# A four-layer graph network on one core: the order of work from a table, layer 1's transposes moved off TensorE

## The chip, the cores and the metric

The kernel runs on one core of a Trainium2 chip. The metric is the device time of one execution in microseconds (us). Engines are named as the profile names them: PE is TensorE (PEld its weight loads), DVE is VectorE, ACT is ScalarE, POOL is GpSimd, and SP is SyncE, which here issues every DMA.

## The reference

64 independent graphs, each with 256 nodes of 256 features (`x`) and a dense 256 x 256 weighted adjacency (`adj`), all fp32, go through four layers. Each layer is followed by x = layernorm(x + layer(x, adj)).

```python
# layer 0, 4 heads of 64
X, q, k = heads(lrelu(x @ W_lin + b_lin)), heads(lrelu(x @ W_q)), heads(lrelu(x @ W_k))
adj_h = adj * sigmoid(q @ k.T / 8);  dis = rsqrt(adj_h.sum(-1))
y = layernorm(concat(dis[:, None] * adj_h * dis[None, :] @ X)) * ln_g + ln_b
# layer 1, 8 heads of 32
attn = softmax(where(adj > 0, q @ k.T / sqrt(32), -9e15))
y = concat(attn @ v) @ Wo + bo
# layer 2
h = silu(rmsnorm((eps * x + adj @ x) @ W1 + b1) * w)      # 1024 wide
y = h @ W2 + b2
# layer 3
Wh = x @ W;  e = where(adj > 0, lrelu(Wh @ a1 + (Wh @ a2).T, 0.2), -9e15)
y = gelu(layernorm(softmax(e) @ Wh) * gamma + beta)
```

## The kernel before

The program is recorded first and emitted afterwards. The function `graph` describes one graph as some 200 operations: each has an engine, a planned cost, the buffers that it reads and writes, and, on PE, a mode (`full`, `rows` or `columns` for matmuls that use the array whole, in row tiles or in column tiles; `transpose`). `Plan.order` then lists the operations of all 64 graphs in one order, with a clock for each engine: it takes, again and again, the ready operation that could start first, where a switch of PE out of a tiled mode is charged with `STAY`. `turn` binds the operations that need an activation table to rounds, and `JOINT` and `join` glue one mean (L680) of an older graph to a score block (L582) of a younger one. `emit` writes the instructions in that order. Every engine runs its own instructions strictly in it, SP its DMA issues too. Several graphs are in flight at different layers, so PE always has another graph's work between two steps of one graph.

Buffers are slots of a few kinds: `s` (512 words a partition), `d` (1024 words, for the exponentials of two heads), `b` (2048, for layer 0's weighted adjacency and layer 2's hidden rows), `c` (small columns), `p` (a PSUM bank, 8 of them), `h` (DRAM).

The places that the text comes back to:

- Layer 0: `feature_major` (L368) makes q and k, `token_major` (L379) the values, L502 the scores in row tiles (four banks), L506 the sigmoids on ACT, L508 the product with `adjT` on DVE, L520 and L524 the degrees (`deg`), L542 the product with the values in column tiles.
- Layer 1: `xT = copy(transposed(x), "xT")` turns x1 on PE (L323, four transposes) and copies it with ACT (L359). L368 makes q and k from it, L379 the values. L582 makes the scores of four heads at a time (two blocks a graph, four PSUM banks each). `softmax` takes a masked minimum of the negated scores with DVE (L465, `low`) and the exp with ACT (L470), which also adds up the row into `r`. DVE transposes the exponentials in 32 x 32 blocks (L603), a DMA writes them to DRAM (L605), four read them back (L607), so that PE needs no transpose for them (but for graph 0). L618 multiplies them with v (`av`). 1/sum goes DVE (L623), PE transpose (L625), ACT copy (L627), DMA to DRAM (L628) and eight broadcast reads (L631) into `rb`, which L635 multiplies into `av`.
- Layer 2: L641 adds eps to the diagonal of `adj2`, L649 sums neighbours, L661 is W1, L666 and L668 take square and scaled copy, L680 the mean over 1024, L685 to L688 the root (`rs`), L693 spreads it (`pr`), L697 multiplies it in, L699 is Silu, L707 is W2.
- Layer 3: `far_transposed` (L335 to L351) turns x3 and the attention through DRAM, L722 is W, L731 and L735 the logits, L746 Gelu; `o` goes out by L749.
- `stats` (L393, L395, L405, L406): for each of the two 128-row halves bn_stats and bn_aggr on DVE, then the inverse root on POOL. `load` (L315) brings x and adj, each as two 1-KB runs a partition.

## Time and profile before

| what | value |
|---|---|
| time of three runs | 2696.8, 2702.2, 2702.13 us (median 2702.13) |
| span of the profiled execution, first to last instruction | 2698.6 us |
| PE, PEld busy | 2666.0, 2144.9 us |
| DVE, ACT, POOL busy | 2436.7, 2228.8, 588.5 us |
| mean granted PE clock | 0.997 |
| DMA | 501 MB, 708045 packets, 67% of 16 engines' span |

The profiled execution's own time is known here as its span; the page gives no other, and it lies within the three runs. Busy time is the union of an engine's instructions, so overlapping ones count once. In a group's row, the mean duration is longer than the spacing of neighbours, because an instruction's end overlaps the next one's start. Idle time in front of an instruction is put down to what released it.

### The profile page before, as it was taken

The page shows a single profiled execution, that of the slowest core. Times are in us where ns is not written, and L with a number is a line of the kernel's source. Part 1 is how long each engine was busy: PE and PEld are TensorE (multiplying, and loading weights), DVE is VectorE, ACT ScalarE, POOL GpSimd, SP SyncE. Part 2 cuts the span into 40 slices and gives each one's busy share as a digit, 9 for nine tenths or more (in the row PEclk, how much of TensorE's full clock was granted, in tenths as well). Part 3 has the DMA queues.
Part 4 walks back from the last instruction along what each step waited for, and adds up shares of the span by engine and source line. Part 5 has one row for each costly group of instructions (what it writes and reads, how often), then busy time and mean ns, then how long its engine had stood idle before and what let it go on. Part 6 is the DMA issues. An engine that isn't in the chain of part 4 may idle for free.

```text
span 2698.6 us, 56499 instructions
## 1 busy us (share of the span) xinstructions
PE 2666.0 (99%) x17568; PEld 2144.9 (79%) x17568; DVE 2436.7 (90%) x7480; ACT 2228.8 (83%) x5343; POOL 588.5 (22%) x902
## 2 busy tenths in 40 slices
...
GB/s 146 133 213 176 219 219 161 211 192 183 200 185 187 215 178 189 196 181 207 202 169 206 186 190 212 173 190 201 172 213 193 169 212 189 186 212 181 169 173 36
DMA packets 708045, 501.01 MB, mean 186 GB/s; under 512 B 309792, under 2 KB 667552, under 8 KB 707744
## 3 DMA queue, kind: packets, MB, share of 16 engines
...
q8 instruction: 140, 2.29, 0.4%
...
## 4 chain that ended last, share of the span: by engine, by line
PE 93%; DVE 3%; ACT 2%; DMA 1%; SPq 1%; issue 1%; POOL 0%; ACTq 0%; POOLq 0%; DVEq 0%
PE ps L368 16%; PE ps L707 16%; PE ps L661 16%; PE ps L379 15%; PE ps L582 5%; PE ps L502 4%; PE ps L542 4%; PE av L618 4%; PE ps L722 4%; PE ps L649 4%; PE ps L323 1%; PE ps L520 1%; PE pr L693 1%; DVE e L465 1%; PE ps L731 0%
## 5 line engine op out<-in xcount | busy, mean ns | idle before, releaser
L470 ACT ACTIVATE e<-e,low 128x256 f32<-128x256 f32 x1152 | 574.6, 500 | 83.7 <-DVE low L465 82.9
L707 PE MATMUL ps<-w,hT 128*128 128x256 f32 x2048 | 466.8, 380 | 1.3 <-ACT hT L699 1.2
L661 PE MATMUL ps<-aggT,w 128*128 128x256 f32 x2048 | 463.4, 380 | 1.6 <-ACT aggT L359 1.0
L707 PEld LDWEIGHTS ps<-w,hT 128*128 128x128 f32 x2048 | 385.7, 190 | 60.4 <-issue 4.6
L661 PEld LDWEIGHTS ps<-aggT,w 128*128 128x128 f32 x2048 | 383.3, 190 | 57.0 <-issue 2.8
L405 POOL TENSOR_SCALAR mv<-mv 128x2 f32<-128x2 f32 x384 | 127.8, 333 | 1316.8 <-DVE mv L395 888.0
L465 DVE CUSTOM_DVE_ANT_0 e<-ps,adj 128x256 f32<-128x256 f32 x1024 | 361.7, 418 | 30.0 <-PE ps L582 29.9
L406 POOL TENSOR_TENSOR mv<-mv,mhalf 128x2 f32<-128x2 f32 x384 | 306.0, 797 | 32.0
L603 DVE STREAM_TRANSPOSE eb<-e 128x1024 f32<-128x1024 f32 x248 | 300.8, 1221 | 0.8 <-ACT e L470 0.7
L668 ACT ACTIVATE hT<-ps,br,r 128x256 f32<-128x256 f32 x512 | 255.7, 585 | 33.9 <-PE ps L707 30.6
L393 DVE BATCH_NORM_STATS2 st<-y 128x6 f32<-128x256 f32 x640 | 238.3, 408 | 1.2
L420 ACT ACTIVATE x<-y,mv 128x256 f32<-128x256 f32 x384 | 215.2, 600 | 28.9 <-DVE mv L416 26.1
L666 ACT ACTIVATE sq<-ps,b 128x256 f32<-128x256 f32 x512 | 220.0, 474 | 20.2 <-PE ps L661 19.7
L470 ACT ACTIVATION_READ_ACCUMULATOR e<-e,low 128x1 f32 x1152 | 219.0, 190 | 0.0
L508 DVE TENSOR_TENSOR att<-att,adjT 128x512 f32<-128x512 f32 x256 | 166.4, 676 | 10.0 <-ACT att L506 10.0
L688 POOL TENSOR_TENSOR rs<-rs,mhalf 128x2 f32<-128x2 f32 x64 | 45.6, 712 | 540.4 <-DVE rs L686 518.9
L528 POOL TENSOR_TENSOR dp<-dp,mhalf 128x8 f32<-128x8 f32 x64 | 110.2, 1722 | 215.8 <-DVE dp L527 168.3
L697 DVE TENSOR_TENSOR hT<-hT,pr 128x1024 f32<-128x1024 f32 x128 | 150.0, 1210 | 5.2 <-PE pr L693 4.3
L582 PE MATMUL ps<-kT,qT 32*128 32x256 f32 x2048 | 146.2, 399 | 0.0
L673 DVE TENSOR_TENSOR sq<-sq 128x512 f32<-128x512 f32 x192 | 129.5, 675 | 11.1 <-ACT sq L666 10.2
L368 PE MATMUL ps<-x0T,w_q 128*128 128x256 f32 x512 | 130.4, 385 | 6.6 <-DMA x0T<-in_xT 6.6
L506 ACT ACTIVATE att<-ps 128x512 f32<-128x512 f32 x256 | 132.2, 603 | 3.8 <-PE ps L502 3.1
...
## 6 DMA issues: line engine op xcount, KB each, us to landing
...
adj<-in_adj SPq DMA_DIRECT2D x128, 256.0 KB, 5.1
...
```

The costliest lines, as they stand in the source:

```text
L368: pe.matmul(two(ps)[:, o, :], w.t[:, k, o * P:(o + 1) * P], two(xT)[:, k, :], start=(k == 0), stop=(k == DB - 1))
L379: pe.matmul(two(ps)[:, n, :], two(xT)[:, k, n * P:(n + 1) * P], w()[:, k, :], start=(k == 0), stop=(k == DB - 1))
L393: op("DVE", 328, lambda n=n: dve.bn_stats(st.t[:, 6 * n:6 * n + 6], two(src)[:, n, :]), [(st, n)], [(src, n)])
L406: pool.tensor_tensor(m()[:, :, 2], m()[:, :, 2], c.mhalf[:, :NB], OP.pow)
L465: op("DVE", 345, lambda n=n: dve.tensor_tensor_reduce(out=E(n), in0=two(logits)[:, n, :], in1=two(negmask)[:, n, :], scale=-scale, scalar= ...
L470: op("ACT", 491, lambda n=n: act.activation(E(n), E(n), AF.Exp, bias=low.t[:, n:n + 1], scale=-1.0, accum_out=r.t[:, col(n):col(n) + 1]), ...
L582: pe.matmul(two(pss[i])[:, n, :], two(qT1)[s, hq, n * P:(n + 1) * P], two(kT1)[s, hq, :], start=True, stop=True)
L603: op("DVE", 1155, lambda e=e, eb=eb: dve.transpose(eb.t.rearrange("p (b g i) -> p g b i", b=4, i=32), e.t.rearrange("p (g b i) -> p g b i" ...
L661: pe.matmul(two(ps)[:, i, :], c.w2_1.t[:, k, (j + i) * P:(j + i + 1) * P], two(aggT)[:, k, :], start=(k == 0), stop=(k == DB - 1))
L666: op("ACT", 357, lambda ps=ps, sq=sq, i=i, j=j: act.activation(two(sq)[:, i, :], two(ps)[:, i, :], AF.Square, bias=c.b2_1.t[:, j + i:j + i ...
L668: op("ACT", 491, lambda ps=ps, i=i, j=j: act.activation(Hb(j + i)[:, 0], two(ps)[:, i, :], AF.Identity, bias=c.br2.t[:, j + i:j + i + 1], ...
L707: pe.matmul(two(ps)[:, n, :], Hb(j)[:, 0, n * P:(n + 1) * P], c.w2_2.t[:, j, :], start=(j == 0), stop=(j == HB - 1))
```

## The change

- `Plan.order` sorts the operations by a key from a table: `TIMES` has one number per operation of a graph, by stage, to which the graph's number times `PERIOD` is added, and for the first and last ten graphs a shift per layer (`SHIFTS`). The clocks remain only to choose the slots. `turn`, `JOINT` and `join` go. Weights have keys of their own.
- Layer 1's input is turned by `far_shuffled`: one DVE transpose in 32 x 32 blocks, one DMA to DRAM in 64-element pieces, four back. Its tokens come in another order, which q's matmul undoes by its access pattern, and which for k is met by an adjacency with columns permuted in the same way (`adjS`, laid out among the inputs). Graph 0 keeps the PE transposes.
- 1/sum is transposed by DVE together with `low`, which now lies in the same tile `r`, and goes to DRAM and back from there; the product with `av` is made in two pieces.
- The exponentials of four heads, not two, share one buffer and one DMA write (kind `D`, three slots; `d` falls from 10 to 4).
- `stats` takes one bn_stats over both halves, interleaved, whose even and odd sums are the two halves; bn_aggr goes, and POOL divides by 256.
- `kT1` gets its bias, in two pieces; L641's two adds become one; the root's eps moves from DVE to POOL.
- x, adj and the output lie in rows of 2 KB, a partition's two halves next to each other.

The diff, cut to its core:

```diff
-WORDS = {"s": 516, "d": 1024, "b": 2048, "c": 32, "p": 512, "h": 1024}
-AHEAD = 12
-STAY = 200
+WORDS = {"s": 516, "d": 1024, "D": 2048, "b": 2048, "c": 32, "p": 512, "h": 2048, "t": 64, "f": 64}
 NEAR = 1, 2, 3
...
-ROUND = 0, 2, 5, 7
-TAIL = 0, 1, 3, 4
-SLOTS = {"s": 42, "d": 10, "b": 3, "c": 72, "p": 8, "h": 8}
+SLOTS = {"s": 46, "d": 4, "D": 3, "b": 3, "c": 48, "p": 8, "h": 8, "t": 4, "f": 8}
+DRAM = "hf"
+
+PERIOD = 43736
+TIMES = {
...
+    "x1": [
+        -22878, -260036, -13056, -13194, -13556, -13246],
...
+SHIFTS = {
+    0: (49484, -2460, -1572, -677, -2727),
+    1: (4489, -16790, -1941, 1285, -26679),
...
+            at = op.time
+            if op.layer is not None:
+                edge = SHIFTS.get(op.graph if op.graph < self.graphs // 2 else op.graph - self.graphs)
+                at += PERIOD * op.graph + (edge[op.layer] if edge else 0)
+            op.at = at if op.at is None else max(at, op.at)
             for nxt in op.after:
+                nxt.at = op.at + 1 if nxt.at is None else max(nxt.at, op.at + 1)
         clock = {e: 0.0 for e in AFTER}
+        free = {k: [(0.0, i) for i in range(n)] for k, n in SLOTS.items()}
+        table, mode, moved = None, "full", 0.0
+        ops = sorted(self.ops, key=lambda op: op.at)
...
+        for op in ops:
+            start = clock[op.engine]
+            if op.engine == "PE":
+                start, mode = start + CHANGE.get((mode, op.mode), 0), op.mode
+            start = max(start, op.ready)
+            op.takes = [v for v in op.values if v.slot is None]
+            for v in op.takes:
+                at, v.slot = free[v.kind].pop(0)
+                start = max(start, at)
+            if op.table is not None and op.table != table:
+                start, table = start + TABLE_LOAD, op.table
             op.start = start
+            end = clock[op.engine] = start + op.cost
...
         v = Value("s", name, 2)
-        op("SP", 470, lambda: nc.sync.dma_start(two(v), t[src][b].rearrange("(n p) d -> p n d", p=P)), [v], after=5000, size=256)
+        op("SP", 500, lambda: nc.sync.dma_start(v.t, t[src][b]), [v], after=5000, size=178)
         return v
...
+    def far_shuffled(src, name):
+
+
+        eb, far, dst = Value("s", "eb"), Value("h", "far"), Value("s", name, 4)
+        op("DVE", 635, lambda: dve.transpose(
+            eb.t.rearrange("p (b k n i) -> p k n b i", b=4, k=2, n=NB),
+            src.t.rearrange("p (n k b i) -> p k n b i", n=NB, k=2, b=4)), [eb], [src])
+        F = lambda: far.t[:32].rearrange("(b k r) (p m) -> b k (r p) m", b=4, k=2, m=64)
+        op("SP", 500, lambda: nc.sync.dma_start(
+            F().rearrange("b k p m -> p (b k) m"), eb.t.rearrange("p (g m) -> p g m", m=64)), [far], [eb], after=2900, size=275)
+        for q in range(4):
+            op("SP", 500, lambda q=q: nc.sync.dma_start(
+                dst.t[32 * q:32 * q + 32].rearrange("j (g m) -> j g m", m=64),
+                F()[q].rearrange("k (a j) m -> j (k a) m", a=4)), [(dst, q)], [far], after=2400, size=69)
...
-        mv, st = Value("c", "mv", 2), Value("c", "st", 2)
+        mv = Value("c", "mv")
         m = lambda: mv.t[:, :6].rearrange("p (n k) -> p n k", n=2)
-        for n in range(NB):
-            op("DVE", 328, lambda n=n: dve.bn_stats(st.t[:, 6 * n:6 * n + 6], two(src)[:, n, :]), [(st, n)], [(src, n)])
-        for n in range(NB):
-            op("DVE", 82, lambda n=n: dve.bn_aggr(m()[:, n, 0:2], st.t[:, 6 * n:6 * n + 6]), [(mv, n)], [(st, n)])
+        op("DVE", 612, lambda: dve.bn_stats(mv.t[:, :6], src.t.rearrange("p (n c) -> p c n", n=NB)), [mv], [src])
...
-            pool.tensor_scalar(m()[:, :, 2], m()[:, :, 1], 1e-5, None, op0=OP.add)
-            pool.tensor_tensor(m()[:, :, 2], m()[:, :, 2], c.mhalf[:, :NB], OP.pow)
-        op("POOL", 1010, fn, [mv], [mv], after=580)
+            pool.tensor_scalar(m()[:, :, 0], m()[:, :, 2], 1.0 / D, 1e-5, op0=OP.mult, op1=OP.add)
+            pool.tensor_tensor(m()[:, :, 0], m()[:, :, 0], c.mhalf[:, :NB], OP.pow)
+        op("POOL", 1060, fn, [mv], [mv], after=580)
...
+    plan.stage("x1 by PE" if b < NEAR[0] else "x1", 1)
+    if b < NEAR[0]:
+        ps, xT = transposed(x), Value("s", "xT", 2)
+        for k in range(DB):
+            op("ACT", 357, lambda ps=ps, k=k: act.copy(
+                two(xT)[:, k, :].rearrange("p (a n i) -> p n a i", n=NB, a=4),
+                two(ps)[:, k, :].rearrange("p (n a i) -> p n a i", n=NB, a=4)), [(xT, k)], [ps])
+    else:
+        xT = far_shuffled(x, "xT")
...
-    xT = copy(transposed(x), "xT")
...
-    kT1 = copy(feature_major(c.w1_k, xT), "kT1")
+    ordered = lambda ap: ap.rearrange("p (a n i) -> p n a i", n=NB, a=4)
+    qk = []
+    for w, bias, name in ((c.w1_q, c.b1_q, "qT1"), (c.w1_k, c.b1_k, "kT1")):
+        ps, y = feature_major(w, xT, ordered if name == "qT1" else lambda ap: ap), Value("s", name, 2)
+        for o in range(2):
+            op("ACT", 357, lambda ps=ps, y=y, bias=bias, o=o: act.activation(
+                two(y)[:, o, :], two(ps)[:, o, :], AF.Identity, bias=bias.t[:, o:o + 1]), [(y, o)], [(ps, o), bias])
+        qk.append(y)
+    qT1, kT1 = qk
...
+        if b >= NEAR[1]:
+            eb, far, eT = Value("D", "eb", 2), Value("h", "far"), Value("D", "eT", 4)
...
-            eb, far, eT = Value("d", "eb"), Value("h", "far"), Value("d", "eT", 4)
-            op("DVE", 1155, lambda e=e, eb=eb: dve.transpose(eb.t.rearrange("p (b g i) -> p g b i", b=4, i=32),
-                                                             e.t.rearrange("p (g b i) -> p g b i", b=4, i=32)), [eb], [e])
-            op("SP", 470, lambda eb=eb, far=far: nc.sync.dma_start(far.t, eb.t), [far], [eb], after=4400, size=512)
-            for q in range(4):
-                op("SP", 470, lambda far=far, eT=eT, q=q: nc.sync.dma_start(
-                    eT.t[32 * q:32 * q + 32].rearrange("j (a g) -> j a g", a=4),
-                    far.t.rearrange("(a j) (b g) -> b j a g", a=4, b=4)[q]), [(eT, q)], [far], after=4400, size=128)
-            eTs.append((eT, lambda i, m, eT=eT: eT.t.rearrange("p (a h n k i) -> p h k n a i", a=4, h=2, n=2, k=2)[:, i, m]))
-
+            op("DVE", 1155, lambda e=e, eb=eb, pair=pair: dve.transpose(
+                eb.t.rearrange("p (b t g i) -> p t g b i", b=4, t=2, i=32)[:, pair],
+                e.t.rearrange("p (g b i) -> p g b i", b=4, i=32)), [(eb, pair)], [e])
+        if b < NEAR[1]:
+            continue
+        op("SP", 500, lambda eb=eb, far=far: nc.sync.dma_start(far.t, eb.t), [far], [eb], after=5500, size=700)
+        for q in range(4):
+            op("SP", 500, lambda far=far, eT=eT, q=q: nc.sync.dma_start(
+                eT.t[32 * q:32 * q + 32].rearrange("j (a g) -> j a g", a=4),
+                far.t.rearrange("(a j) (b g) -> b j a g", a=4, b=4)[q]), [(eT, q)], [far], after=5000, size=178)
+        for u in range(2):
+            eTs.append((eT, lambda i, m, eT=eT, u=u: eT.t.rearrange("p (a u h n k i) -> p u h k n a i", a=4, u=2, h=2, n=2, k=2)[:, u, i, m]))
...
-    op("DVE", 180, lambda: dve.reciprocal(r.t[:, :16], r.t[:, :16]), [r], [r])
-    ps = Value("p", "ps")
-    op("PE", PE_TR, lambda ps=ps: pe.transpose(ps.t[:16, :P], r.t[:, :16], c.ident), [ps], [r], mode="transpose")
-    rT, far, rb = Value("s", "rT"), Value("h", "far"), Value("s", "rb", H1)
-    op("ACT", 160, lambda ps=ps: act.copy(rT.t[:16, :P], ps.t[:16, :P]), [rT], [ps])
-    op("SP", 470, lambda far=far: nc.sync.dma_start(far.t[:2].rearrange("q (g m) -> (q g) m", m=P), rT.t[:16, :P]),
-       [far], [rT], after=2000, size=8)
+    op("DVE", 160, lambda: dve.reciprocal(r.t[:, :16], r.t[:, :16]), [(r, 0)], [(r, 0)])
+    rT, far, rb = Value("c", "rT"), Value("f", "far"), Value("s", "rb", H1)
+    op("DVE", 122, lambda: dve.transpose(rT.t, r.t), [rT], [r])
+    op("SP", 500, lambda far=far: nc.sync.dma_start(far.t[:64].rearrange("x (k i) -> (x k) i", k=2), rT.t), [far], [rT], after=2500, size=26)
     for h in range(H1):
-        op("SP", 470, lambda h=h, far=far: nc.sync.dma_start(
-            two(rb)[h % 4 * HD1:(h % 4 + 1) * HD1, h // 4, :],
-            far.t[h // 4:h // 4 + 1, h % 4 * N:(h % 4 + 1) * N].to_broadcast([HD1, N])), [(rb, h)], [far], after=1700, size=32)
-    yT = Value("s", "yT")
-    op("DVE", 575, lambda: dve.tensor_tensor(yT.t, av.t, rb.t, OP.mult), [yT], [av, rb])
+        op("SP", 500, lambda h=h, far=far: nc.sync.dma_start(
+            two(rb)[h % 4 * HD1:(h % 4 + 1) * HD1, h // 4, :].rearrange("p (a m) -> p a m", a=4),
+            far.t[:64].rearrange("(a h) m -> h a m", a=4)[h][None].to_broadcast([HD1, 4, 64])),
+            [(rb, h)], [far], after=2100, size=35)
+    yT = Value("s", "yT", 2)
+    for n in range(NB):
+        op("DVE", 345, lambda n=n: dve.tensor_tensor(
+            two(yT)[:, :, n * P:(n + 1) * P].rearrange("p q (a i) -> p q a i", a=4),
+            two(av)[:, :, n * P:(n + 1) * P].rearrange("p q (a i) -> p q a i", a=4),
+            rb.t.rearrange("p (q a n i) -> p q n a i", q=2, n=NB, a=4)[:, :, n], OP.mult), [(yT, n)], [av, rb])
...
     adj2 = load("adj2", "adjT")
-    for n in range(NB):
-        d = lambda n=n: two(adj2)[:, n, n * P:(n + 1) * P]
-        op("DVE", 200, lambda d=d: dve.tensor_tensor(d(), d(), c.eps_id.t, OP.add), [(adj2, n)], [(adj2, n), c.eps_id])
+    d = lambda: adj2.t.rearrange("p (g w) -> p g w", g=4)[:, ::3]
+    op("DVE", 305, lambda: dve.tensor_tensor(d(), d(), c.eps_id.t[:, None, :].to_broadcast([P, NB, P]), OP.add),
+       [adj2], [adj2, c.eps_id])
...
-    rs = Value("c", "rs")
-    pm = lambda sq=sq: sq.t[:, N:N + 64]
-    op("DVE", 125, lambda ps=ps: dve.transpose(pm(), ps.t[:, :64]), [(sq, 1)], [ps])
-    op("DVE", 50, lambda: dve.tensor_scalar(
-        rs.t[:, :NB], pm().rearrange("p (n k) -> p n k", k=32)[:, :, 0], 1e-6, None, op0=OP.add), [rs], [(sq, 1)])
-    op("POOL", 700, lambda: pool.tensor_tensor(rs.t[:, :NB], rs.t[:, :NB], c.mhalf[:, :NB], OP.pow), [rs], [rs])
+    rs = Value("t", "rs")
+    root = lambda: rs.t.rearrange("p (n k) -> p n k", n=NB)[:, :, 0]
+    op("DVE", 163, lambda ps=ps: dve.transpose(rs.t, ps.t[:, :64]), [rs], [ps])
+
+    def fn():
+        pool.tensor_scalar(root(), root(), 1.0, 1e-6, op0=OP.mult, op1=OP.add)
+        pool.tensor_tensor(root(), root(), c.mhalf[:, :NB], OP.pow)
+    op("POOL", 1060, fn, [rs], [rs], after=580)
...
-    for name in ("x", "adj"):
-        given[name + "T"] = given[name].swapaxes(-1, -2)
+    rows = lambda a: a.reshape(-1, 2, P, 256).swapaxes(1, 2).reshape(-1, P, 512)
+    adj = given["adj"]
+    given["xT"], given["adjT"] = rows(given["x"].swapaxes(-1, -2)), rows(adj.swapaxes(-1, -2))
+    given["adjS"] = rows(adj.reshape(-1, 256, 2, 4, 32).swapaxes(2, 3).reshape(-1, 256, 256))
+    given["x"], given["adj"] = rows(given["x"]), rows(adj)
```

## The prediction

> **What bounds the kernel now.** I read the busy shares first, then the chain of waits, a middle stretch, the PE timeline, and the groups that the change touches. From the page:
>
> ```profile
> PE 2666.0 (99%) x17568; PEld 2144.9 (79%) x17568; DVE 2436.7 (90%) x7480; ACT 2228.8 (83%) x5343; POOL 588.5 (22%) x902
> PE 93%; DVE 3%; ACT 2%; DMA 1%; SPq 1%; issue 1%; POOL 0%; ACTq 0%; POOLq 0%; DVEq 0%
> ```
>
> PE is busy 99% of the span and is 93% of the chain that ended last. A busy PE need not be at its peak, so I looked inside. The middle, as busy time by stretch (PE, PEld, DVE, ACT, POOL, clock, DMA share, GB/s):
>
> ```profile
> 960.00:1290.00 330.00, 330.00 (x2186) 266.61 (x2185) 305.64 (x937) 277.13 (x666) 72.97 (x112) 1.00 0.70 192
> ```
>
> A middle graph takes 273 PE passes (144 full, 72 in column tiles, 48 in row tiles, 9 transposes), so 2186 are 8 graphs: 41.2 us a graph, no idle PE, DVE working 38.2 of them. The PE timeline shows what a pass and a change of mode cost (start, duration; the difference of two starts is the cost):
>
> ```profile
> 1007.84 1.89 PE L707 MATMUL ps<-w,hT 128*128 128x256 f32 x8
> 1009.66 2.00 PE L502 MATMUL ps<-qT,kT 64*128 64x256 f32 x16
> 1011.58 0.28 PE L625 MATMUL ps<-ident,r 128*16 128x128 f32 x1
> 1011.70 3.62 PE L661 MATMUL ps<-aggT,w 128*128 128x256 f32 x16
> ...
> 1024.87 0.60 PE L323 MATMUL ps<-ident,x 128*128 128x128 f32 x4
> 1025.31 1.03 PE L379 MATMUL ps<-w_l,x0T 128*128 128x256 f32 x4
> ```
>
> L661: 16 passes in 3.45 us, 216 ns each. L323: 4 transposes in 0.44 us, 109 each. L707: 8 x 216 = 1.73, yet 1.82 until L502: 93 ns to enter a tiled mode. L502: 16 passes, two at a time, 1.73, yet 1.92: 0.2 us to leave. Doing this over the whole trace by the program's order splits the span: 6.6 us until the first matmul, 2542.7 streaming (full 4610 pairs x 432 ns; tiled ones divided by the tiles side by side; 668 transposes x 109), 95.5 changes of mode (median of each pair of kinds), 38.4 waiting (half of it in the first and last 100 us[...]), 15.4 after the last matmul. Sum 2698.6. So time falls with PE's passes and changes of mode, as long as nothing else becomes late.
>
> [...] 93 ns into a tiled mode, 137 to 150 out of column tiles, 200 to 213 out of row tiles, only 25 between column tiles of one size. [...] starts of neighbours lie 326 ns apart for bn_stats of 256 elements, while a 512-element add takes 602, not twice a 256-element one (335). [...] SP has a wait of L607 for far, 64 us in all.
>
> **The change part by part.**
>
> *PE.* Rows concerned:
>
> ```profile
> L323 PE MATMUL ps<-ident,x 128*128 128x128 f32 x268 | 42.1, 279 | 0.2 <-ACT x L420 0.2
> L625 PE MATMUL ps<-ident,r 128*16 128x128 f32 x64 | 17.7, 277 | 0.0
> ```
>
> Layer 1's input loses 4 transposes in 63 graphs (graph 0 keeps them), 252; the sums lose 64. 316 x 109 ns = 34.4 us, all on PE: streaming 2542.7 to 2508.2. The order: PE's runs of one mode fall from 969 to 622 (full 372 to 156, transposes 263 to 138, tiled ones nearly the same). Tiled blocks now stand behind each other and are left into a neighbour: entries from full fall from 237 to 140. Pricing every neighbouring pair in the new order with the median of that pair before gives 82.3 us instead of 95.5. The pair column-to-row (out of 64-column tiles, 53 times) isn't in the trace before; it gets the 139 ns that other column-to-row pairs took. Bounds: 25[...] (-6), and 300, as much as entering and leaving (+8.5).
>
> *Head.* SP now issues w0_k, a 128-KB row, the 1-MB W1 and five more ahead of the first x0T: 2.3 MB up to it instead of 0.77. The first 16 us moved 273 GB/s (that stretch); 1.5 MB more is +5.5 us. PE has nothing before it. Bounds: 0, if later waits there shrink by as much, and +8.
>
> *DVE.* Six statistics a graph turn from two bn_stats and two bn_aggr (2 x 326 + 2 x 88) into one bn_stats over interleaved halves. No trace has that form; from the 512-element operations I take 610, -0.22 each, -1.3 a graph. Bounds: 590, and 1200 if the 1-KB stride halves it (+2.2 a graph). Added: x1's transpose 0.63 (row eb<-x) and 1/sum's 0.12; the product with 1/sum in two pieces +0.1, the two eps adds as one -0.1, rs one less -0.07. Sum -0.65: 38.1 of 41.2 becomes about 37.5.
>
> *ACT.* Without xT (0.48) and rT (0.16), kT1 with bias in two pieces +0.25: 34.6 to 34.2 us a graph; 249 table loads instead of 252. *POOL* +0.3 us a graph, on 22%: nothing, hidden by its idle time, while rs waits 15 us for PE's use of it.
>
> *SP and DMA.* e goes in two 1-MB halves: 20 issues a graph become 10; x1 adds 5: 57 to 52, 0.45 us each, 23 us of a graph. Inputs in 2-KB rows halve those packets. x1 and 1/sum move in 256-byte pieces, which before has not; landing bounded by 2.0 and 5 us (rows of far and in_adj); taken 3. Off the path, if the order leaves room, which is the point.
>
> **Does the new order leave room?** It repeats each graph. I walked one period by hand, times after the start of a graph's second score block (second half of its heads), with the spacings above. PE: scores, values (eT.v) and layer 0's product until 4.7, layer 0's scores at 4.7, pr 6.6, W2 at 8.6, W1 at 13.8, layer 1's q and k at 22.4 and 24.1, first score block at 32.0, next second block at 40.5. (1) Layer 0's scores take the four PSUM banks of the second score block, freed by eight DVE minima. DVE reaches them 0.7 after the block's statistics, frees the second bank by 2.9 and the fourth by 3.6; PE needs them at 4.7 and 5.6: room 1.8. (2) DVE then works 25.9 us and is at deg at 29.4, PE gives it at 31.9. (3) ACT ends the exps at 6.9, sigmoids at 10, Silu at 17.6, the copies of k at 28.3 and of W1's outputs at 30; the first score block needs both at 32: room 1.7. (4) x1: transposed at 4.8, written by 8, read behind yT's four reads, landed at 14.7; q needs it at 22.4: room 7.7. (5) e's last half is written at 12.4, landed at 29, needed at 41.5. (6) the three 2048-word buffers come free at the eT.v product and are first filled after it. So PE needn't wait, and no stall replaces the removed ones; late next would be (3), then (1).
>
> **Sum.** 12.1 + 2508.2 + 82.3 + 38.4 + 15.4 = 2656.4 us of span, against 2698.6: -42. The median of the three runs shown, 2702.1, is 3.5 above the profiled span, so 2660 us.
>
> **The rivals.**
> *DVE or ACT takes over* (slower). Room in (1) and (3) is under 2 us, on hand-added spacings; DVE has only 40.5 - 37.5 = 3.0 us a graph to stand still. For: it is already 92% busy; ACT waits for DVE 0.1 us here and there (e <- low, 83 us in all), and a fixed order can't step aside. Against: before, DVE stood still 3.1 us a graph without holding PE. The gain of 42 us is 0.66 a graph; it decides when standing still passes 3.7 us. At 4.8 (or with the stride bound of bn_stats, 37.5 + 3.5) a graph takes 42.2: 2660 + 64 x 1.7 = 2770; just over the edge some 2710.
> *The waits eat the gain*: 0.5 us a graph at (1), (3) or behind SP, whose longest waits were 24 to 29 us for DVE; 2692.
> *Ends tighten too*: the head and tail orders hold fewer waits, 38 becoming 20, and the late first load costs nothing: 2636.
> *It doesn't do what it says*: PE order is in the program[...].
>
> **How the numbers follow.** Forecast 0.60 (2645 to 2680), tighter ends 0.18, waits eat most 0.09 of which 0.03 land within 0.2% (about what a measurement of this kernel can tell from no change), DVE or ACT takes over 0.13. Faster 0.60 + 0.18 + 0.06 = 0.84; same 0.03; slower 0.13. Range 2634 to 2698: it leaves out the slower case and little below.
>
> **What would show it.** Right: transposes of x only in graph 0 and the last three; a middle stretch with 268 passes in 40.5 us and PE without gaps; the first matmul near 12 us; bn_stats of one half-interleaved row at 0.6 us spacing; waits of PE only at the ends. Wrong: PE idle before layer 0's scores (bank, on DVE) or before the first score block (ACT); DVE at 95% or more; q of layer 1 waiting for DMA; bn_stats near 1.2 us.

## The result, and the profile after

| | before | after |
|---|---|---|
| median of four runs | 2700.45 us | 2815.28 us (2811.79 to 2817.03) |
| ratio | | 1.0426, 95% interval 1.0411 to 1.044 |
| span of the profiled execution | 2698.6 us | 2813.9 us |

The change makes the kernel 4.3% slower; 2660 us was forecast. First the page of the changed kernel: busy times, then the chain that ended last.

```profile
PE 2652.4 (94%) x17252; PEld 2143.6 (76%) x17252; DVE 2441.4 (87%) x6391; ACT 2192.5 (78%) x5278; POOL 603.8 (21%) x966
PE 46%; DMA 25%; DVE 19%; SPq 5%; ACT 3%; issue 3%; DVEq 0%; POOLq 0%; ACTq 0%; POOL 0%
DMA eT<-far 14%; PE ps L700 8%; PE ps L384 8%; PE ps L748 8%; PE ps L395 8%; DVE e L479 4%; DVE eb L633 4%; DMA far<-rT 4%; SPq L664 3%; PE av L654 3%; PE ps L557 2%; PE ps L517 2%; DMA far<-eb 2%; PE ps L610 2%; PE ps L766 2%
```

PE's matmuls are the 17252 that the forecast had counted (316 fewer), but the chain is no longer PE's: from 93% it fell to 46%, and a quarter of the span is DMA, most of it `eT<-far`, the reads of transposed attentions. The busy shares alone would mislead: DVE (90 to 87%) and ACT (83 to 78%) take a smaller share than before, and still PE is held. Below is the middle stretch (PE, PEld, DVE, ACT, POOL, clock, DMA share, GB/s):

```profile
960.00:1290.00 330.00, 312.22 (x2072) 252.44 (x2072) 290.07 (x775) 260.30 (x634) 73.86 (x118) 0.99 0.78 194
```

PE stands still for 18 us of 330, and 2072 passes are 7.7 graphs of 268, 42.7 us each. Over thirty middle graphs, from the first transpose of one graph's exponentials to the next graph's, the mean is 43.2 us (before: 41.3). PE's timeline tells where the gap stands in each graph:

```profile
1363.19 1.89 PE L395 MATMUL ps<-w_l,x0T 128*128 128x256 f32 x8
1366.68 1.96 PE L395 MATMUL ps<-v,eT 128*128 128x256 f32 x8 [1.60 <-DMA eT<-far]
1368.58 1.15 PE L610 MATMUL ps<-kT,qT 32*128 32x256 f32 x16
1370.68 1.93 PE L654 MATMUL av<-eT,v 128*32 128x256 f32 x32 [0.96 <-ACT x L433]
```

The second L395 is layer 3's product of v3 with its transposed attention (`eT3` in the code). It starts 3.5 us after the product before it instead of 1.7 (8 passes of 216 ns), and behind it in PE's order stand layer 1's second score block (L610) and the values product (`av`, L654). Splitting PE's span as the prediction did gives 13.1 us to the first matmul, 2508.2 streaming, 193.6 waiting, and 99.0 for changes of mode and the end. By the profile's rows PE stood 84.6 us ahead of v3 x eT3 and 31.2 ahead of av. The DMA issues (KB each, median us from issue to landing; the 64-KB row of `eT` is eT3, the 256-KB row is layer 1):

```profile
far<-eb SPq DMA_DIRECT2D x124, 1024.0 KB, 5.6
eT<-far SPq DMA_DIRECT2D x496, 256.0 KB, 6.6
xT<-far SPq DMA_DIRECT2D x496, 64.0 KB, 2.3
eT<-far SPq DMA_DIRECT2D x244, 64.0 KB, 8.0
far<-rT SPq DMA_DIRECT2D x64, 16.0 KB, 4.0
```

x3, which is read in the same way and size as eT3, lands in 2.5 us (median; the row of 2.3 holds x1's reads too); eT3 takes 8.0 (before: 2.5). Its place in SP's timeline says why (start, time to issue, count):

```profile
1343.95 0.38 SPq L638 DMA_DIRECT2D far<-eb  x1
...
1344.90 1.04 SPq L638 DMA_DIRECT2D far<-eb  x1
1348.42 3.14 SPq L664 DMA_DIRECT2D rb<-far  x6
1351.61 2.80 SPq L640 DMA_DIRECT2D eT<-far  x6
1354.51 1.20 SPq L345 DMA_DIRECT2D eT<-far  x2
1356.28 0.30 SPq L640 DMA_DIRECT2D eT<-far  x1
1357.39 2.46 SPq L345 DMA_DIRECT2D eT<-far  x2
1359.99 2.25 SPq L640 DMA_DIRECT2D eT<-far  x1
```

Both 1-MB writes of a graph (L638) go out within a microsecond, then all eight 256-KB reads (L640), with eT3's four (L345) among them. In the trace the first five big reads land at 1356.26, 1357.38, 1358.73, 1359.97 and 1361.16: one every 1.2 us, 214 GB/s. eT3's last read lands at 1366.55, and PE starts at 1366.68.

This closes a loop. In the chain of waits of the same stretch (start, us, what) one round can be followed from yT to av:

```profile
1331.25 0.35 DVE yT L670
...
1334.73 3.38 DVE eb L633 x3
...
1344.42 3.94 DMA far<-rT
...
1352.55 6.17 DMA eT<-far
...
1358.74 7.80 DMA eT<-far
...
1366.68 1.98 PE ps L395 x8
```

Transposes, writes, reads, v3 x eT3, scores, av, then yT (which needs av), and behind yT in DVE's order the next graph's transposes. The round must fit into a graph's PE work, and it doesn't. Two buffers tie into it. The third transpose writes into a buffer that `av` has just read, by the program's choice of slots; in the trace it starts 5.7 us after yT, which needs av too, so DVE's order and not this buffer holds there, though no run moved yT. And on DVE itself L505 (layer 0's values) stands:

```profile
DVE v L505 <- PE ps L610: 76.9, 20, 6.4
DVE v L505 <- DMA out<-o: 41.1, 12, 5.3
```

In most graphs L505 fills a buffer that the write of the output `o` must first free, and that write is issued behind the reads (L798, 1365.17, landed at 1369.79; L505 starts at 1369.89). Of 127 us that DVE stood there, 118 ended within 0.3 us of that landing, whoever the row names. And `av` takes the PSUM bank that L505 frees. So a late clump of reads holds PE in two ways: through eT3, and through the output write, L505 and av.

### The profile page after: what moved, and what is told of

It reads as the page before. It is cut to its first block, busy times and chain, and to the rows that moved or that the text cites. A ratio compares the mean times of both kernels' runs of the same rounds, so it can differ in the third digit from the quotient of the medians.

```text
span 2813.9 us, 54722 instructions
## 1 busy us (share of the span) xinstructions
PE 2652.4 (94%) x17252; PEld 2143.6 (76%) x17252; DVE 2441.4 (87%) x6391; ACT 2192.5 (78%) x5278; POOL 603.8 (21%) x966
## 4 chain that ended last, share of the span: by engine, by line
PE 46%; DMA 25%; DVE 19%; SPq 5%; ACT 3%; issue 3%; DVEq 0%; POOLq 0%; ACTq 0%; POOL 0%
DMA eT<-far 14%; PE ps L700 8%; PE ps L384 8%; PE ps L748 8%; PE ps L395 8%; DVE e L479 4%; DVE eb L633 4%; DMA far<-rT 4%; SPq L664 3%; PE av L654 3%; PE ps L557 2%; PE ps L517 2%; DMA far<-eb 2%; PE ps L610 2%; PE ps L766 2%
## 5 line engine op out<-in xcount | busy, mean ns | idle before, releaser
L484 ACT ACTIVATE e<-e,r 128x256 f32<-128x256 f32 x1024 | 506.0, 496 | 18.1 <-DVE r L479 17.4
L419 POOL TENSOR_TENSOR mv<-mv,mhalf 128x2 f32<-128x2 f32 x384 | 331.2, 863 | 32.1
L707 ACT ACTIVATE hT<-ps,br,r 128x256 f32<-128x256 f32 x512 | 315.4, 625 | 0.0
L408 DVE BATCH_NORM_STATS2 mv<-y 128x6 f32<-128x512 f32 x320 | 222.3, 695 | 6.6
L395 PE MATMUL ps<-v,eT 128*128 128x256 f32 x512 | 141.9, 426 | 84.6 <-DMA eT<-far 41.9
L395 PEld LDWEIGHTS ps<-v,eT 128*128 128x128 f32 x512 | 102.7, 209 | 117.8 <-issue 31.0
L484 ACT ACTIVATION_READ_ACCUMULATOR e<-e,r 128x1 f32 x1024 | 192.3, 188 | 0.0
L523 DVE TENSOR_TENSOR att<-att,adjT 128x512 f32<-128x512 f32 x256 | 166.1, 674 | 14.1 <-ACT att L521 14.1
L740 ACT ACTIVATE hT<-hT 128x1024 f32<-128x1024 f32 x128 | 130.0, 1051 | 40.3 <-DVE hT L738 38.6
L654 PE MATMUL av<-eT,v 128*32 128x256 f32 x2048 | 126.7, 388 | 31.2 <-ACT x L433 20.8
L505 DVE TENSOR_TENSOR v<-ps,b_l 128x512 f32<-128x512 f32 x64 | 44.1, 690 | 127.2 <-PE ps L610 76.9
L610 PE MATMUL ps<-kT,qT 32*128 32x256 f32 x2048 | 152.0, 409 | 1.1 <-ACT kT L596 1.1
```

The lines of the kernel that those rows point to most:

```text
L395: pe.matmul(two(ps)[:, n, :], two(xT)[:, k, n * P:(n + 1) * P], w()[:, k, :], start=(k == 0), stop=(k == DB - 1))
L408: op("DVE", 612, lambda: dve.bn_stats(mv.t[:, :6], src.t.rearrange("p (n c) -> p c n", n=NB)), [mv], [src])
L419: pool.tensor_tensor(m()[:, :, 0], m()[:, :, 0], c.mhalf[:, :NB], OP.pow)
L484: op("ACT", 491, lambda n=n: act.activation(E(n), E(n), AF.Exp, bias=L(n), scale=-1.0, accum_out=r.t[:, col(n):col(n) + 1]), [(e, part(n)) ...
L654: pe.matmul(two(av)[i * HD1:(i + 1) * HD1, hq, :], two(v1)[:, m, h * HD1:(h + 1) * HD1], eTs[h // 2][1](i % 2, m), start=(m == 0), stop=(m ...
L707: op("ACT", 452, lambda ps=ps, i=i, j=j: act.activation(Hb(j + i)[:, 0], two(ps)[:, i, :], AF.Identity, bias=c.br2.t[:, j + i:j + i + 1], ...
```

## Experiments

Each run is compared with the kernel before on the same chip. The times within a round are medians over thirty middle graphs, worked out from each trace, counted from the start of a graph's first transpose of exponentials; the period is the mean from there to the next graph's. "PE waits" is the same split as above, over the whole span. A blank stands where the trace lacks landings of that read.

| run | us | first write | first read | last landing | period | PE waits |
|---|---|---|---|---|---|---|
| changed kernel | 2815.3 | 8.5 | 17.0 | 32.6 | 43.2 | 194 |
| e3_reads_first | 2846.1 | 8.8 | 19.6 | 32.6 | 43.7 | 223 |
| y3_behind_scores | 2819.4 | 8.5 | 17.0 | 32.5 | 43.2 | 193 |
| rT_reads_last | 2877.9 | 9.2 | 16.2 | 34.6 | 43.9 | 262 |
| rT_on_POOL | 2816.8 | 8.6 | 16.9 | 32.4 | 42.7 | 194 |
| loads_behind_reads | 2843.2 | 7.8 | 15.7 | 33.0 | 43.6 | 217 |
| reads_in_1KB | 2801.1 | 9.6 | 18.1 | 33.3 | 42.0 | 182 |
| writes_ahead | 2803.3 | 5.8 | 16.5 | 32.4 | 42.7 | 190 |
| writes_far_ahead | 2844.4 | 2.4 | 16.6 | 32.5 | 42.8 | 224 |
| writes_ahead_rT_on_POOL | 2762.6 | 5.7 | 14.0 | 30.4 | 40.9 | 148 |
| eT3_a_period_later | 2744.0 | 5.6 | 13.9 | 28.3 | 40.7 | 120 |
| x1_by_PE | 2714.0 | 5.9 | 14.1 | 29.6 | 40.8 | 63 |
| e3_by_PE | 2693.6 | 7.2 | 16.1 | 29.2 | 40.8 | 44 |
| e3_by_PE_with_empty_issues | 2700.4 | 8.6 | 16.6 | | 40.8 | 52 |
| twelve_empty_issues_ahead | 2747.9 | 11.6 | 19.5 | | 41.4 | 99 |

The theories, in short: A, later called L, is the round above, one sum of latencies through queue, DMA and engines; B, later R, is the DMA engines' rate, bytes alone; C is the order of DVE or ACT. The edits to the table name the operation's stage; in the diffs a number is the key within `TIMES`.

### Is it eT3's place among the reads?

Edit of e3_reads_first (the four reads of eT3 issued ahead of the eight):

```diff
     "e3": [
-        225632, 186632, 248234, -95896, 188509, 303747, 315177, 308934, 314526],
+        225632, 186632, 248234, -95896, 188509, 294599, 294599, 294599, 294599],
```

> The changed kernel with one edit in the table: the four reads of layer 3's transposed attention (64 KB each, in 128-byte pieces) stand on SP's queue ahead of the eight 256-KB reads of layer 1's attention, not among and behind them. Nothing is added or removed. Theory A (a loop through the DMA queue: v3 x eT3 on PE opens layer 1's second score block, whose exponentials, transposes, writes and reads stand in one queue with the next eT3): eT3 lands some 3 us after issue instead of 8.0, PE no longer waits for it, and the wait moves to av, which needs layer 1's reads; of the 2.8 us a graph some 1.5 to 2.5 are won, 2655 to 2725 us. Theory B (the 16 DMA engines' rate is the bound, whatever the order): the same bytes, 2800 to 2830. Theory C (DVE's or ACT's order holds PE, and eT3 only happens to be last): under 20 us won, 2795 to 2820.

Measured 2846.14 us, ratio to before 1.0548 (1.053 to 1.0565). eT3 did land as hoped:

```profile
eT<-far SPq DMA_DIRECT2D x244, 64.0 KB, 2.5
```

That is outside the ranges of all three theories. The big reads began 2.6 us later, the last landing stayed at 32.6 us, and PE now stood 120 us ahead of av. A saw the move of the wait but not its size. The reads' landing is only part of what held av: 66 of the 120 us ended as L505 freed its bank, and L505 had stood for the output write behind the reads:

```profile
DVE v L505 <- DMA out<-o: 120.7, 31, 6.5
```

Bringing eT3 forward alone buys nothing, as long as all the reads, and what is queued behind them, end as late.

y3_behind_scores puts the score block ahead of v3 x eT3 on PE:

```diff
     "y3": [
-        333821, 231651, 225040, 337186, 347307, 141236, 74504, 323745, 319142, 172218],
+        335100, 231651, 225040, 337186, 347307, 141236, 74504, 323745, 319142, 172218],
```

> The changed kernel with one edit in the table: on PE the product v3 x eT3 stands behind the second score block, between it and av, instead of ahead of both. No operation and no DMA is changed; PE changes mode twice more a graph (some 0.15 us). Theory A1 (eT3 holds the score block, and with it the exponentials, the transposes and the writes that eT3 itself then queues behind): the loop is cut, 2670 to 2720 us. Theory A2 (the loop closes through av, then yT, which stands ahead of the transposes in DVE's order, whoever waits first): av still stands behind eT3 and waits as long, 2790 to 2840 us. Theory B (rate of the DMA engines): 2800 to 2840.

Measured 2819.36 us, 1.0439 (1.0424 to 1.0455): the same period, the same waits. A1 falls; A2 and B both allow it. Here too most of the wait ahead of av (51 of 60 us) ended as L505 freed the bank, so this run does not show that av waited for its own reads.

### Take a path out of DRAM

e3_by_PE, the transposes put where PE had just been busy with W1:

```diff
     "e3": [
-        225632, 186632, 248234, -95896, 188509, 303747, 315177, 308934, 314526],
+        312200, 186632, 248234, -95896, 188509, 303747, 315177, 308934, 314526],
...
-    eT = copy(transposed(e), "eT") if b >= plan.graphs - NEAR[2] else far_transposed(e, "eT3")
+    eT = copy(transposed(e), "eT")
```

> The changed kernel with layer 3's attention transposed by PE for every graph instead of through DVE and DRAM: 61 x 4 transposes of 109 ns (27 us) and some 61 x 0.2 us of mode changes more on PE, one ACT copy of 0.47 us a graph more, one DVE transpose and eight DMAs a graph less. Theory A: the wait for eT3 is gone and PE's order is otherwise the same, av waits instead for a part: 2690 to 2760 us. Theory B (DMA rate): 8 of some 74 KB-sized issues and the 128-byte packets (4 of 36 us of DMA time a graph) are gone, 2700 to 2790 as well, but with DMA landings of layer 1's reads unchanged above 6 us. Theory C: 2830 to 2870, the added PE work on top.

x1_by_PE:

```diff
+    "x1 at PE": [0, 0, 0],
...
-    plan.stage("x1 by PE" if b < NEAR[0] else "x1", 1)
-    if b < NEAR[0]:
+    plan.stage("x1 by PE" if b < NEAR[0] else "x1 at PE", 1)
+    if True:
```

> The changed kernel with one part undone: layer 1's input is transposed by PE for every graph and copied by ACT in two halves, instead of through DVE and DRAM. Paid on PE: 63 x 4 transposes of 109 ns (27.5 us) and some 10 us of mode changes; on ACT two copies of 0.36 us a graph. Gone: one write and four reads a graph, five SP issues (2.2 us) and some 3.4 us of DMA time in 256-byte pieces, all queued shortly ahead of the attention's writes. Theory A (loop): the waits shrink by 2 to 3 us a graph, 2680 to 2760 us in all. If eT3's own pieces alone make the loop, the waits stay and the added PE work comes on top or fills them: 2810 to 2860.

Measured 2693.61 us, 0.9985 (0.9977 to 0.9993), and 2714.02 us, 1.0051 (1.0036 to 1.0066): 122 and 101 us under the changed kernel, although each gives PE 27 us of transposes back. The same middle stretch of e3_by_PE:

```profile
960.00:1290.00 330.00, 330.00 (x2202) 270.50 (x2195) 305.36 (x813) 280.79 (x671) 77.97 (x125) 1.00 0.73 197
```

PE is without a gap, and DVE and ACT work more than in the changed kernel without holding it. So the amount of their work is not the cause (theory C); DVE's stand at L505 fell from 127 to 7 us with the rest. x1_by_PE is the telling one: its eT3 still took 8.0 us to land, and the waits fell from 194 to 63 us. So eT3's small pieces alone do not make the loss; these two runs, with 3.0 and 3.4 us less to the last landing, end most of it. Each also takes a DVE transpose of 0.7 us out of the stretch between yT and the transposes, which is part of the round.

The control before_with_e3_by_PE makes the same replacement in the kernel before:

```diff
-    eT = copy(transposed(e), "eT") if b >= plan.graphs - NEAR[2] else far_transposed(e, "eT3")
+    eT = copy(transposed(e), "eT")
```

> A control: the kernel before, with layer 3's attention transposed by PE for all graphs, as in the run e3_by_PE. Theory A (in the kernel before eT3's reads land in 2.5 us and hold nothing, so that only the changed kernel gains from this edit): the 27 us of added transposes and their changes of mode are paid in full, 2715 to 2750 us. Theory B (the DMA engines' rate costs time in the kernel before as well): 2660 to 2700.

Measured 2754.51 us, 1.0203 (1.0188 to 1.0218): 55 us slower, just over the range. Of that 27 us are the added transposes, 5 changes of mode and some 21 more waiting; the greedy list chooses another order around the added operations, and what waits there is left open. The kernel before gains nothing from it: its reads of layer 1 land 13 us or more before they are needed (below). Set against 2693.61 it shows what else the change holds: with layer 3's attention on PE in both, the changed kernel is 61 us faster.

### The stand for 1/sum, and the loads

SP waits in the changed kernel (us in total, times, longest):

```profile
SPq L664 <- DMA far<-rT: 165.4, 64, 4.1
SPq L351 <- DMA far<-eb: 164.7, 63, 5.2
```

SP stands 2.6 us a graph for the write of 1/sum just ahead of the big reads (the 3.9 us of the expectations are that write's time to landing). rT_reads_last moves six of the eight reads of 1/sum behind the reads of the attention:

```diff
     "layer 1": [
-        -292171, -332905, -463540, -325283, -585287, 54654, -66521, -251318, -276322, -295456, -30216, 56307,
+        -292171, -332905, -463540, -325283, 41400, 54654, 41400, 41400, 41400, 41400, 41400, 56307,
```

> The changed kernel with one edit in the table: the eight broadcast reads of 1/sum (rb) follow layer 1's attention reads on SP's queue, so that SP no longer stands 3.9 us a graph waiting for the small write of 1/sum before it issues those reads. Theory A (loop through SP's queue): the reads start 1.5 to 3 us a graph earlier and PE's wait for eT3 shrinks as much unless the later rb then holds DVE; 2690 to 2770 us. Theory B (DMA rate): the reads start earlier and land no earlier, 2800 to 2830. Theory C: 2795 to 2820.

Measured 2877.85 us, 1.0664 (1.0641 to 1.0687), wrong under all theories. The key put them between the big reads, ahead of the last ones: the first read gained 0.8 us, the last landed 2.0 us later. rT_on_POOL changes the issuing engine of the nine DMAs (the write's key becomes 41156, and the two late reads now follow it too):

```diff
-    op("SP", 500, lambda far=far: nc.sync.dma_start(far.t[:64].rearrange("x (k i) -> (x k) i", k=2), rT.t), [far], [rT], after=2500, size=26)
+    op("POOL", 500, lambda far=far: pool.dma_start(far.t[:64].rearrange("x (k i) -> (x k) i", k=2), rT.t), [far], [rT], after=2500, size=26)
...
-        op("SP", 500, lambda h=h, far=far: nc.sync.dma_start(
+        op("POOL", 500, lambda h=h, far=far: pool.dma_start(
```

> The changed kernel with the nine DMAs of 1/sum (one write, eight broadcast reads, 16 and 32 KB) issued by POOL instead of SP; the bytes, pieces and destinations are the same. SP's queue loses nine issues of 0.43 us a graph and the 3.9 us stand for the write of 1/sum; POOL, 21% busy, gets them behind its other work. Theory A-issue (the loop closes through SP's queue in order: issue times and standing count): the reads of layer 1's attention start some 2 to 4 us a graph earlier and the waits go, 2650 to 2700 us. Theory A-rate (within the loop the 16 DMA engines are saturated from the transposes to the last read, so that only bytes count): the bytes stay, 2780 to 2830. If POOL issues much slower than SP, or its rb lands late, yT holds DVE: 2720 to 2780.

Measured 2816.81 us, 1.0447 (1.0425 to 1.0469): no change, as A-rate had it. The issue time taken off SP bought nothing, because the stand moved. SP's wait in this run:

```profile
SPq L640 <- DMA far<-eb: 439.3, 62, 9.1
```

SP now stands 7.1 us a graph for the landing of the 1-MB writes. The two paths to the first read end within 0.8 us of each other: in the changed kernel the second write lands at 16.2 us and SP is free at 17.0; here both are at 16.9.

loads_behind_reads and loads_after_all_reads move the loads of x and x's transpose, which stood ahead of the writes:

```diff
     "layer 0": [
-        -319197, -113134, -100311, -71943, -247582, -546773, -546197, -131479, -172183, -152737, -281181, -565681,
+        -308488, -113134, -89808, -71943, -247582, -546773, -546197, -131479, -172183, -152737, -281181, -565681,
```

> The changed kernel with one edit in the table: the loads of x and of its transpose (256 KB each), which stand on SP's queue just ahead of the writes of layer 1's attention, are issued behind that attention's reads instead; both are needed more than 20 us later. Nothing else is touched. Theory A (a loop of fixed latencies through SP's queue and the DMA engines, in which everything queued between the transposes and the last read counts): two issues of 0.45 us and 512 KB leave the loop, 1 to 2 us a graph: 2690 to 2760 us. Theory B (rate over the whole graph): the bytes are the same, 2800 to 2830.

In loads_after_all_reads the two keys are -296652 and -77972.

> The run loads_behind_reads in fact set the two 256-KB loads behind six of the eight attention reads, ahead of the last two and of three reads of eT3. Here they stand behind all of them, ahead of the two late rb reads. Theory A-issue: two issues of 0.45 us leave the loop, 0.9 us a graph: 2740 to 2790 us. Theory A-rate: 512 KB leave the loop, about 1.3 us a graph at the 400 GB/s seen there: 2720 to 2770 us. Theory B (rate over the whole graph): 2800 to 2830.

Measured 2843.17 us, 1.0531 (1.051 to 1.0552), and 2962.85 us, 1.0985 (1.0969 to 1.1001). Neither edit did what was meant, and both lie outside all their ranges. In the first the loads stand behind only six of the eight reads and delay the last ones. In the second PE ran into the load itself:

```profile
PE ps L395 <- DMA x0T<-in_xT: 169.2, 48, 8.7
```

"More than 20 us later" was read off keys, not off times. They tell nothing between the theories, but something on tables: a key is a rank, not a time.

### Issue time or bytes?

e3_by_PE_with_empty_issues and twelve_empty_issues_ahead add DMAs of 4 bytes to e3_by_PE, four ahead of the writes and four among the reads, or twelve ahead of the writes:

```diff
+    for _ in range(8 if b < plan.graphs - NEAR[2] else 0):
+        pad = Value("c", "pad")
+        op("SP", 500, lambda pad=pad: nc.sync.dma_start(pad.t[:1, :1], t["x"][b][:1, :1]), [pad], after=2000, size=1)
```

> The kernel of e3_by_PE (2694 us) with eight DMAs of 4 bytes a graph that nothing reads, at the places on SP's queue where the eight DMAs of eT3 stood: the issue time is put back, the bytes (512 KB a graph, half of them in 128-byte pieces) are not, nor does anything wait for eT3. Theory A-issue: 3.5 us a graph of SP's time are back in the loop, waits return in good part: 2740 to 2830 us. Theory A-rate: 2690 to 2705.

> A dose: the kernel of e3_by_PE with twelve DMAs of 4 bytes a graph that nothing reads, all directly ahead of the two 1-MB writes on SP's queue (12 x 0.43 = 5.2 us of issue time, no bytes). Theory L: 29.2 us to the last landing become some 34, and with 10.7 us to the next transpose 44.5 us a graph, over the 41.3 us of PE work of that kernel: 2830 to 2900 us. The run with four ahead and four among the reads (2700 us) stayed under that edge. Theory R: 2690 to 2710.

Measured 2700.37 us, 1.001 (1.0002 to 1.0019), and 2747.86 us, 1.0182 (1.0167 to 1.0197). Issues alone, with hardly any bytes, do lengthen the round, past an edge: the first read went from 16.1 to 16.6 (7 us more in all) and to 19.5 (54 us). The first result is within A-rate's range and not A-issue's; the second is outside both, over R's by 38 us and under L's by more than 80, the latter perhaps because, without eT3, the round does not pass through v3 x eT3 and the scores (1366.68 to 1370.68, 4 us), but from the last read straight to av; that was not tested.

writes_ahead moves four writes and two loads behind the 1-MB writes, writes_far_ahead also the reads of x1 and of layer 0's output. Shown is writes_ahead:

```diff
     "e3": [
-        225632, 186632, 248234, -95896, 188509, 303747, 315177, 308934, 314526],
+        225632, 294601, 294601, 294601, 294601, 303747, 315177, 308934, 314526],
...
     "layer 0": [
-        -319197, -113134, -100311, -71943, -247582, -546773, -546197, -131479, -172183, -152737, -281181, -565681,
+        -317703, -113134, -99023, -71943, -247582, -546773, -546197, -131479, -172183, -152737, -281181, -565681,
...
     "layer 1": [
-        -292171, -332905, -463540, -325283, -585287, 54654, -66521, -251318, -276322, -295456, -30216, 56307,
+        -292171, -332905, -463540, -325283, 32190, 54654, 32190, 32190, 32190, 32190, 32190, 56307,
```

(the second block's big reads get 32195, so that they stay behind). writes_far_ahead adds:

```diff
     "x1": [
-        -22878, -260036, -13056, -13194, -13556, -13246],
+        -22878, -260036, -11551, -11551, -11551, -11551],
...
     "y0": [
-        -87831, -373130, -729274, -232310, -329503, -339824, -34600, -122314],
+        -87831, -373130, -55287, -55287, -55287, -55287, -34600, -122314],
```

> The changed kernel with edits in the table alone: the two 1-MB writes of layer 1's attention are moved on SP's queue ahead of the two 256-KB loads of x and its transpose and of the four writes of layer 3's attention (six issues of 0.43 us), which follow them, ahead of the rb reads. Theory L (one loop a graph: transposes, SP's queue, writes, reads, landing, then av, yT and the next transposes; in the changed kernel 32.6 us from the first transpose to the last landing and 10.7 us on to the next first transpose, 43.3 us against 40.5 us of PE work): the first write is issued some 2.6 us earlier, the last read lands after 30 to 31 us, 40.7 to 41.7 us a graph: 2660 to 2730 us. Theory R (the DMA engines' rate, bytes alone): the same bytes between the first write and the last read's landing, the writes share the engines with the loads: 2790 to 2820.

> As writes_ahead, and the four reads of x1 and the four of layer 0's output, which stood on SP's queue ahead of the writes too (one of them waiting there for its own write to land), follow the writes as well. Theory L: the first write is issued 4 to 5 us earlier than in the changed kernel, the last read lands at 28 to 29 us, under the edge: 2650 to 2690 us, unless x1 or layer 0's output, which land some 5 us later, then hold PE: 2700 to 2750.

Measured 2803.33 us, 1.039 (1.0364 to 1.0417), and 2844.39 us, 1.054 (1.0522 to 1.0559). The first write moved by 2.7 and 6.1 us as meant, the first read by 0.5: what was moved still stood ahead of the reads. In writes_far_ahead the later x1 also held PE (35 us). The total of writes_ahead is within R's range, and L failed in both, unless the first read was simply held by SP's second path, its other issues. Both edits together test that:

> The edits of writes_ahead and of rT_on_POOL together. Alone, each left the first read of layer 1's attention where it was, 16.5 to 17 us after the first transpose: with the writes ahead they had landed at 13.2, but SP stood for 1/sum and its other issues until 16.5; with 1/sum on POOL SP was free, but the writes landed at 16.9. Theory L (the longer of the two paths sets the first read, then 15.6 us of reads, then 10.3 us to the next transpose): the first read at 13 to 14 us, the last landing at 29 to 30, 39.5 to 40.3 us a graph, under the 40.5 us of PE work: 2645 to 2690 us. Theory R (within the loop the bytes set the last landing, wherever they stand): the last landing stays at 32 us, 2780 to 2820.

Measured 2762.58 us, 1.0235 (1.0218 to 1.0252). One edit alone was worth 12 us and the other none; together they are worth 53. The first read moved to 14.0, the last landing to 30.4, and the period to 40.9. Theory R, under which the last landing can't move with the same bytes, falls; writes_ahead had met it because of the second path. L's total was missed: the period of 40.9 us is at the edge of 40.5, not under it, and 148 us of waits are left. The same with writes_far_ahead:

> The edits of writes_far_ahead and of rT_on_POOL together. Theory L: the first read at 11 to 13 us, the last landing at 27 to 29: the loop has slack, but the reads of x1 and of layer 0's output, which are later, held PE in writes_far_ahead (some 45 us at the first products of layers 0, 1 and 3 in the order there): 2670 to 2730 us. Theory R: 2800 to 2840.

Measured 2807.58 us, 1.04 (1.0366 to 1.0434): the first read again at 14.1, the period 40.9 in the middle, and the earlier writes bought nothing; x1 and layer 0's output, which land later, held PE elsewhere.

### The size of the pieces, and a period more for eT3

reads_in_1KB cuts each big read in two, with 1-KB pieces as before the change:

```diff
+            for z in range(2):
+                op("SP", 500, lambda far=far, eT=eT, q=q, z=z: nc.sync.dma_start(
+                    eT.t[32 * q:32 * q + 32].rearrange("j (a z g) -> z j a g", a=4, z=2)[z],
+                    far.t.rearrange("(a j) (b z g) -> b z j a g", a=4, b=4, z=2)[q, z]), [(eT, 2 * q + z)], [far], after=5000, size=90)
```

> The changed kernel with each 256-KB read of layer 1's attention cut into two of 128 KB, whose pieces are 1 KB as in the kernel before, not 2 KB; the writes stay 1 MB. Eight issues of 0.43 us a graph more on SP, spread among reads. While these reads run, a 2-KB packet took 167 ns (83 ns a KB) in the changed kernel and a 1-KB packet 66 ns in the kernel before. If the size of the pieces makes that difference: 2 MB take 8.4 instead of 10.7 us of the 16 engines, the last read lands some 2 us earlier, 41 to 42 us a graph: 2690 to 2750 us. If the rate is set by the direction, the rows read or the neighbours: packets of 80 ns and more, 2810 to 2850.

Measured 2801.14 us, 1.0371 (1.035 to 1.0393): outside both ranges, 14 us less than the changed kernel, and not at the reads: the last landing came 0.7 us later, while PE's stand ahead of av fell from 31.2 to 7.5 us. With another issue order the program gave L505 another buffer, and DVE stood there 8 us instead of 127, none of it for the output write; the loss stayed all the same, now ahead of v3 x eT3 (98 us). So the output write is not the whole of it. In the trace a 1-KB packet took 83 ns on the mean, as much per KB as the changed kernel's 2-KB packets of 167 ns. So the piece size is not what slows the reads.

eT3_a_period_later adds to writes_ahead_rT_on_POOL (with three more 516-word buffers, 49, and 22 small ones instead of 48):

```diff
+    "y3 late": [377557, 275387, 268776, 380922, 391043, 184972, 118240, 367481, 362878, 215954],
+    "out late": [378677, 396838, 394978, 413163, 499838, 497398, 490641],
+    "e3 late": [225632, 294601, 294601, 294601, 294601, 318752, 318752, 318752, 318752],
...
+    last = last or (" late" if b < plan.graphs - 12 else "")
     plan.stage("e3" + last, 3)
```

> The kernel of writes_ahead_rT_on_POOL (2763 us; first read at 14.0, last landing at 30.4 us after the first transpose, 10.0 us more to the next), and for the first 52 graphs layer 3's transposed attention is read behind layer 1's reads instead of among them, and v3 x eT3 with what follows it runs one graph period later at the same places; three more 516-word buffers hold what lives longer. PE's, DVE's and ACT's work is the same, the bytes of a period too. Theory L: 256 KB of small pieces leave the stretch of reads, which took 13.1 us without them in e3_by_PE: last landing at 27 to 28 us, 37 to 38 us for the loop, 2.5 us under the 40.5 us of PE work, so that the waits that were left go as well: 2650 to 2680 us, under the kernel before. Theory R (rate over the period): the last landing moves less than 1 us, 2750 to 2800.

Measured 2743.95 us, 1.0176 (1.0156 to 1.0195). Two stretches, the middle and one near the end:

```profile
1290.00:1620.00 330.00, 329.57 (x2174) 270.12 (x2173) 310.73 (x810) 277.66 (x666) 117.48 (x195) 1.00 0.82 209
2300.00:2500.00 200.00, 189.07 (x1235) 152.28 (x1233) 185.80 (x489) 163.36 (x386) 74.22 (x124) 0.99 0.78 201
```

In the middle the forecast stands: 40.7 us a graph, PE all but without gaps, with all transposes off PE and a DMA share of 0.82, higher than in the changed kernel (0.79 in this stretch). So neither the DMA engines' bytes nor DVE's and ACT's work sets the period. The last big read landed at 28.3 us, eT3 at 29.1, now for the next period. The total, outside both ranges, does not stand: PE idles 17 us between 100 and 300 us and 11 us in the second stretch shown. The first and last graphs follow shifts of their own, which no edit here was fitted to; that this is the rest was not tested.

### The old way of ordering

new_ops_greedy_order keeps the changed operations and buffers, and puts back the kernel before's `Plan.order` with `turn`, `JOINT` and `join`:

> All of the changed operations (one bn_stats, x1 and 1/sum through DVE and DRAM, 1-MB transfers, 2-KB rows, the buffers), but their order is chosen by the greedy list of the kernel before instead of by the table. Theory A (the table's SP order makes the loss, the operations are good): near or under the kernel before, 2650 to 2715 us, PE waits under 80 us. Theory B (the operations' DMA work makes the loss): 2770 to 2840, with DMA landings as long as in the changed kernel.

Measured 3094.94 us, 1.1475 (1.1454 to 1.1496), far outside both ranges. PE's longest waits there (L391 makes q and k, L402 the token-major products, L774 layer 3's W):

```profile
PE ps L391 <- DMA xT<-far: 90.5, 29, 6.5
PE ps L402 <- DMA eT<-far: 78.6, 31, 8.7
PE ps L774 <- DMA xT<-far: 40.2, 10, 6.8
```

The list was never fitted to these operations, nor the numbers of buffers to the list, so this does not say how good the table is, or which of the two makes the loss. It does show that these operations with these buffers, under an order that worked for the old ones, bring a loss: PE waits for what comes back from DRAM, and an order must leave the time for it. Of all runs, e3_by_PE is the fastest; its 0.15% under the kernel before is less than the 0.2% by which the four runs of the kernel before lie apart.

## Why the prediction was wrong

- **PE's sum was right.** Streaming was 2508.2 us as forecast, the first matmul came at 13.1 us instead of 12.1, and the changes of mode and the end took 99.0 instead of 97.7. x is transposed on PE in graph 0 and the last three only, as the group with 16 of them shows below.
- **The waits failed**: 38.4, carried over from the kernel before, were forecast and 193.6 measured, 155 us of the 157.5 by which the span missed.
- **The step that failed is the walk, item (5).** In its frame, from the start of the second score block, it had the last half written at 12.4, landed at 29 and needed at 41.5, 12.5 us of room. Measured: written at 18.9, landed at 42.0. Part of this is the loop feeding on itself; in e3_by_PE, where PE hardly waits, it is still 15.0 and 36.0. Two things were left out: the first transpose, which the table sets behind yT, comes at 6.8 there, so that all four stand in one clump; and the reads, which then run one behind the other at 214 GB/s. In the kernel before the same work was spread out: first transpose at 0.5, first read at 10.0 while later transposes still ran, last landing at 31.2. And its av came a graph later, 71.9 us after the second score block (median) where the changed kernel's comes at 44.9: the reads had landed 42 us ahead of it in the median graph and 13 at the least, against 3.0 now.
- **eT3 was not walked at all**, nor the output write behind those reads, whose landing frees L505's buffer and with it av's bank. eT3 is read among those reads, and PE needs it 4 us ahead of av. That the table put both there could be read from the program.
- **"Late next would be (3), then (1)"** was wrong. Neither layer 0's scores nor the copies of k held PE (0.9 and 1.1 us in their rows). Of the 31.2 us ahead of av, 22.5 ended as L505 freed av's bank: a bank that DVE freed late, as (1) feared, but at av, and because L505 itself stood for the output write.
- **The two costs bounded from both sides** were as taken. The row of bn_stats over interleaved halves has 695 ns on the mean, like the 512-element adds (683 to 690), so the stride cost nothing. x1's 256-byte pieces landed in 2.1 us (median), 3 taken, and q of layer 1 did not wait for them. x1's way through DRAM cost time all the same: without it (x1_by_PE) the kernel took 101 us less.
- **DVE's fall by 0.65 us a graph** did not show: 2441.4 us busy against 2436.7, though the rows of bn_stats and bn_aggr fell from 403 to 267 us. Where it went is left open. ACT's 34.2 us a graph was right (2192.5 / 64 = 34.3).
- **The rivals**: "DVE or ACT takes over" named the wrong limit, and its sum does not close (37.5 + 4.8 is 42.3, 37.5 + 3.5 is 41.0, where it has 42.2 for both); "the waits eat the gain" the right place, SP, at a fifth of the size (32 us). Both asked how long an engine may stand. Neither asked how long one graph's data is under way.

The groups meant above (line, engine, tiles; busy us, mean ns; idle before and its releasers):

```profile
L323 PE MATMUL ps<-ident,x 128*128 128x128 f32 x16 | 2.7, 283 | 0.1
L408 DVE BATCH_NORM_STATS2 mv<-y 128x6 f32<-128x512 f32 x320 | 222.3, 695 | 6.6
L395 PE MATMUL ps<-v,eT 128*128 128x256 f32 x512 | 141.9, 426 | 84.6 <-DMA eT<-far 41.9 <-DMA rb<-far 13.0 <-DVE xb L444 6.5
```

The last row also shows how a wait for several things is booked on several names: only 41.9 of the 84.6 us stand under eT.
